# A graph kernel of two layers: epilogue operations of slabs 1 to 6 placed a step sooner or later, and other steps without partial sums

## The chip, the cores and the metric

The kernel runs on one core of a Trainium2 chip. The metric is the device time of one execution in microseconds (us). Before the change it is 233.94 us (median of three runs, 233.77 to 235.03). The engines are called PE (TensorE), DVE (VectorE), ACT (ScalarE), POOL (GpSimd) and SP (SyncE).

## The reference, cut to what matters

x has 4096 rows of 64, adj is 4096 x 4096 with zeros and ones.

```python
# layer 0
support = x @ W0
rank = cumsum(adj, axis=1); deg = rank[:, -1:]
k = minimum(deg, 100); pos = rank - (deg - k)
w = adj * where(pos > 0, 0.5 ** (k - pos), 0)
x1 = layernorm(x + w @ support + b0)
# layer 1
deg1 = maximum(sum(adj, axis=1) + 1, 1)
h = (adj @ x1 + x1) / deg1
z = concat([x1, h], axis=1) @ W1 + b1
u = relu(z); u = u / maximum(norm(u, axis=1), 1e-12)
out = layernorm(x1 + u)
```

So every one of the 16.8 million entries of adj is used three times: for a count of ones to its right, for a weight 0.5 to the power of that count, and for the plain sum of neighbours in layer 1. Layer 1 of any row needs x1 of all its neighbours, in all slabs.

## The kernel before, in words

The 4096 rows are cut into 8 slabs g of 512 rows, and the 4096 columns into 8 blocks k of 512, so there are 64 steps (g, k). Within a slab the blocks go from k = 7 down to 0, because the count runs from the right. Step i is numbered 0 to 63; slab g has steps 8g to 8g + 7. One load per step (512 KB in SBUF, issued on POOL's queue, line 109, converted to bf16 on its way) brings the transposed block of adj into one of 33 buffers `a16`. A buffer becomes free when its four matmuls of layer 1 are done.

A step's work for layer 0, `weigh`: 16 matmuls with `tri` (line 351) and 16 with `mine` (line 360) fill two PSUM tiles `v`, the exponents; ACT turns the first half and DVE the second half into the bits of bf16 weights `w` (lines 367 and 368, 1.1 and 1.2 us). `gather` (line 378, four matmuls) multiplies them with x, kept as high and low halves in fp16. It runs one step behind: `held` is the step before. The running count is made a chunk of steps ahead: `count` (line 321), then a DVE addition to the count so far (`cs`, lines 331 and 333), a matmul that spreads it over the partitions (`rep`, line 339), and an ACT operation (`near`, line 341) whose result `mine` reads. A chunk is one step in slabs 0 to 2, one or two in slab 3, two in slab 4, four in slabs 5 and 6, and two, two, four in slab 7.

Layer 1 begins long before layer 0 is done: `some_sums` takes, in each step, up to QUOTA = 4 matmuls (line 387; called a unit here) from a list `todo`, which `jobs` spells out: a pair (g, [k...]) says that slab g's sum over these blocks is made in one go in one PSUM bank. The first sum of a slab is copied out by ACT (line 406), later ones are added by DVE (line 403). The sums of one slab over block k need x1 of slab k, with the flag `low_at` telling from which step. No unit is issued in the steps of SAVED. The list is worked off in order: an entry that isn't ready holds back all behind it.

When a slab's last gather is done its epilogue runs, spread over the next steps as hooks. `at(i, engine, fn, g)` places a function at a step and an engine's slot, and the table PLACES (line 39) overrides step and slot by name. In the program, a step runs in this order: hooks of ACT, one load, hooks of POOL, the counts, hooks "DVE, early", `weigh`, hooks "ACT, late", the unit, `spread`, the eviction of a partial sum, `gather`, `first_hT`, hooks of PE, hooks of DVE. Each engine executes its instructions in program order.

The epilogue of slabs 2 to 6 (HALVED): `first_hT` copies the gathered sum (line 477), `half_sum` adds its low half (481), `half_high`, `half_rest` (488), `half_low` split it into fp16 parts in `x1T`, `half_degree` and `half_degree_out` (499) count the row's neighbours, `half_pz` multiplies by W0 and W1 (505), `half_y` adds x and an early part of layer 1 (510, 512). Then for all slabs: `first_mv` (bn statistics, 456 and 458), `first_s` (root, 427), `first_r` (four small operations, 433 to 437), `half_scale` (516), `first_x1` (four tensor_scalar operations that normalise, 565, on POOL for slabs 0 to 3 and on DVE for the others), `first_hi` (570), `first_xl` (575), `first_lo` (578), which split x1 for layer 1, `first_least` (552, 553), and `half_b1` (523), `half_c1` (527), `half_c1_b1` (531) on POOL. Slabs 0 and 1 transpose x1 instead, by `first_px` (583), `first_x1T` (586), `first_pu`, `first_c1`, `times_degree`.

At the start, `split_x` (221, 223 on POOL) and `split_x_low` (226 on DVE) split a block of x in each of steps 0 to 7, and `prepare` (229, 230 on POOL) scales W0, which has to have been loaded. After step 63 comes a tail in an order written out by hand, which ends the program. The change leaves that order as it is.

The slots of a step, in the code:

```python
run(i, ACT); load_next(); run(i, POOL)
for s in share: count(*s, s == ahead[0], s == ahead[-1])
run(i, "DVE, early")
w = w or weigh(g, k, nr)
run(i, "ACT, late")
done = some_sums(i, 0 if i in SAVED else QUOTA)
# at a chunk's last step: half of gather(*held) if no unit was issued, then spread
if done is not None: evict_part(done)
# rest of gather(*held); first_hT at a slab's first step
run(i, PE); run(i, DVE)
```

Of the kernel before, what the change touches and what calls it, by code (L numbers as in the profile page):

```python
# [17 lines left out]
PE = mybir.EngineType.PE  # L18
ACT = mybir.EngineType.Activation
DVE = mybir.EngineType.DVE  # L20
POOL = mybir.EngineType.Pool
# [14 lines left out]
QUOTA = 4  # L36
EARLY = 3
HALVED = range(2, 7)
PLACES = {"centered_parts": (9, POOL), "prepare": (5, POOL), "bias_columns": (7, POOL), "prepare_wx": (10, POOL), "half_c1_b1 3": (38, POOL), "half_c1_b1 4": (46, POOL), "half_c1_b1 5": (57, POOL), "half_c1_b1 6": (62, POOL), "products_parts": (10, POOL), "first_mv 0": (10, "DVE, early"), "first_r 0": (11, "DVE, early"), "first_least 0": (13, "DVE, early"), "first_s 0": (11, ACT), "first_pu 0": (16, PE), "times_degree 0": (18, POOL), "first_least 1": (20, DVE), "first_pu 1": (24, PE), "first_mv 2": (28, DVE), "first_s 2": (29, ACT), "first_r 2": (29, DVE), "half_scale 2": (29, DVE), "first_x1 2": (30, POOL), "first_hi 2": (31, ACT), "first_xl 2": (31, POOL), "first_lo 2": (32, ACT), "first_least 2": (31, DVE), "half_high 2": (26, ACT), "half_rest 2": (26, DVE), "half_degree_out 2": (26, DVE), "half_degree 2": (26, PE), "half_low 2": (27, ACT), "half_pz 2": (27, PE), "half_y 2": (27, DVE), "first_x1 3": (37, POOL), "first_hi 3": (38, "ACT, late"), "first_least 3": (38, "DVE, early"), "half_low 3": (34, ACT), "half_b1 3": (38, POOL), "half_c1 3": (37, POOL), "first_s 4": (44, ACT), "half_scale 4": (45, "DVE, early"), "first_xl 4": (46, POOL), "first_least 4": (45, DVE), "first_lo 4": (47, "ACT, late"), "half_low 4": (42, ACT), "half_b1 4": (46, POOL), "first_s 5": (52, ACT), "half_scale 5": (53, DVE), "first_hi 5": (54, "ACT, late"), "first_least 5": (57, DVE), "half_low 5": (50, ACT), "half_b1 5": (52, POOL), "half_c1 5": (55, POOL), "first_s 6": (60, ACT), "first_xl 6": (62, POOL), "first_lo 6": (62, "ACT, late"), "half_low 6": (58, ACT)}
LAG = 1  # L40
SAVED = (15, 17, 18, 21, 27)


@with_exitstack
def adj_resnorm_kernel(
# [23 lines left out]
    nc = tc.nc  # L69
# [317 lines left out]
        nc.tensor.matmul(acc, lhsT=x1hl[:, b, :], rhs=A[g][b // KB][:, b % KB, :], start=first, stop=last)  # L387


    jobs = [(0, [0]), (1, [0]), (0, [1]), (2, [0, 1]), (1, [1]), (3, [1, 0, 2]), (1, [2]), (0, [2]), (2, [2]), (4, [2, 1, 0, 3]), (1, [3]), (2, [3]), (0, [3]), (5, [3, 2, 1, 0, 4]), (3, [3, 4]), (6, [4, 3, 2, 1, 0, 5]), (4, [4, 5]), (1, [4, 5]), (0, [4, 5]), (2, [4])]  # L390
    acc1 = {}

    todo = [(g, k * KB + q, (k, q) == (ks[0], 0), (k, q) == (ks[-1], KB - 1)) for g, ks in jobs for k in ks for q in range(KB)]
# [14 lines left out]
    def some_sums(i, n):  # L408

        done = None  # L410
        while n and todo and done is None and ready(i, todo[0][0], todo[0][1]):
            g, b, first, last = todo.pop(0)
            if first:
                acc1[g] = ps_a.tile([P, R], F32, tag="acc1", name=f"acc_part_{g}_{b}")
            second(acc1[g], g, b, first, last)
            n -= 1
            if last:
                done = g
        return done
# [140 lines left out]

    def first_x1(g):
        mv, y, r = ep["mv", g], ep["y", g], ep["r", g]
        by = nc.gpsimd if g in [0, 1, 2, 3] else nc.vector
        for t in range(TB):
            by.tensor_scalar(  # L565
                x1[:, g * TB + t, :], y[:, t, :], mv[:, t, 0:1], r[:, t : t + 1], ALU.subtract, ALU.mult
            )
# [40 lines left out]
    def at(i, engine, fn, *args):  # L608
        i, engine = PLACES.get(" ".join([fn.__name__, *map(str, args)]), (i, engine))
        hooks[i, engine].append((fn, args))  # L610
# [35 lines left out]
    for g in range(NG - 1):  # L646
        i = NK * (g + 1)
        easy = POOL if g < EARLY else DVE
        late = 1 if g in HALVED else 0
# [3 lines left out]
            (3, "ACT, late", first_s, g),  # L653
            (3, DVE, first_r, g),
            (4, easy, first_x1, g),
            (5, ACT, first_hi, g),
            (5, easy, first_xl, g),
# [53 lines left out]
    for c, chunk in enumerate(chunks):  # L711
# [4 lines left out]
        for (g, k), share in zip(chunk, shares):  # L716
# [13 lines left out]
            n_todo = len(todo)  # L730
            done = some_sums(i, 0 if i in SAVED else QUOTA)
            half = 0
# [335 lines left out]
```

## Time and profile before

| what | value |
|---|---|
| median of three runs | 233.94 us (233.77, 233.94, 235.03) |
| the profiled execution's own time | 233.72 us |
| its span | 231.7 us |
| mean granted clock of PE | 0.975 |
| PE busy | 209.5 us (90%), 3138 instructions |
| DVE busy | 182.2 us (79%) |
| ACT busy | 140.6 us (61%) |
| POOL busy | 112.3 us (48%) |
| loads of adj, share of the 16 DMA engines | 73.7% |
| first weigh of step 16 / 32 / 40 | 55.45 / 99.33 / 122.40 us |
| the last load of adj lands | 174.75 us |

An engine's busy time leaves out waiting at its front, and matmuls are pipelined, with their ends modelled; a PE that is busy all the time is not necessarily at its peak. Shares over the whole span mix the 64 steps with a start and a tail that have other limits, so a step is read from its own stretch of the trace: from the first matmul of line 351 of one step to that of the next. In rows of the timeline the columns are start, duration (of one instruction, or of a run of equal ones), engine, line, operation, output and inputs, sizes, how many, and in brackets the idle time of the engine before it with what ended it.

### The profile page before, as it was taken

The page shows a single profiled execution, that of the slowest core. Times are in us where ns is not written, and L with a number is a line of the kernel's source. Part 1 is how long each engine was busy: PE and PEld are TensorE (multiplying, and loading weights), DVE is VectorE, ACT ScalarE, POOL GpSimd, SP SyncE. Part 2 cuts the span into 40 slices and gives each one's busy share as a digit, 9 for nine tenths or more (in the row PEclk, how much of TensorE's full clock was granted, in tenths as well). Part 3 has the DMA queues.
Part 4 walks back from the last instruction along what each step waited for, and adds up shares of the span by engine and source line. Part 5 has one row for each costly group of instructions (what it writes and reads, how often), then busy time and mean ns, then how long its engine had stood idle before and what let it go on. Part 6 is the DMA issues. An engine that isn't in the chain of part 4 may idle for free.

```text
span 231.7 us, 7494 instructions
## 1 busy us (share of the span) xinstructions
PE 209.5 (90%) x3138; PEld 95.2 (41%) x3178; DVE 182.2 (79%) x454; ACT 140.6 (61%) x212; POOL 112.3 (48%) x211
## 2 busy tenths in 40 slices
PE   7589999998998999999999999999999999999910
PEld 2133445443533443334333433443334344776810
DVE  6459877997797789798975996687678866599983
ACT  6057886687778767686557455664675451142684
POOL 7439677761537081641584056325433040079970
PEclk9799999999999999999999999999999999999975
DMA  6999999999999999999999999999970000000013
GB/s 201 209 213 219 215 216 213 217 217 214 215 219 212 214 214 223 211 214 214 218 217 207 200 183 210 204 195 181 205 168 4 3 0 0 3 0 1 23 45 113
DMA packets 11984, 37.36 MB, mean 161 GB/s; under 512 B 1328, under 2 KB 3504, under 8 KB 11952
## 3 DMA queue, kind: packets, MB, share of 16 engines
q0 software_dynamic: 9216, 33.56, 73.7%
q1 hardware_dynamic: 2736, 3.34, 4.7%
q8 instruction: 24, 0.39, 0.6%
q14 instruction: 8, 0.07, 0.1%
HBM read 69.40 MB, written 1.05 MB: 304 GB/s over the span
## 4 chain that ended last, share of the span: by engine, by line
PE 40%; DVE 11%; POOL 4%; ACT 3%; issue 2%; ACTq 0%; DVEq 0%; POOLq 0%
PE acc L378 12%; PE acc_part L387 11%; PE v L351 5%; PE cnt L321 3%; PE v L360 3%; ACT u L961 2%; POOL scratch L947 2%; DVE w L368 2%; POOL scratch L978 2%; DVE cs L331 1%; PE rep L339 1%; PE va L930 1%; PE pz L505 1%; PE vb L387 1%; DVE part L403 1%
## 5 line engine op out<-in xcount | busy, mean ns | idle before, releaser
L367 ACT ACTIVATE w<-v,less 128x1024 int16<-128x1024 f32 x64 | 71.3, 1113 | 43.7 <-PE v L360 31.7
L368 DVE TENSOR_SCALAR w<-v 128x1024 int16<-128x1024 f32 x64 | 78.2, 1221 | 13.0 <-PE v L360 12.1
L378 PE MATMUL acc<-w,xhl 128*128 128x512 bf16 x235 | 65.2, 380 | 1.9 <-issue 1.1
L109 POOL DMA_DIRECT2D a<-in_adjT_dram x64 | 36.9, 622 | 48.2 <-PE acc_part L387 25.4
L387 PE MATMUL acc_part<-a,x1hl 128*128 128x512 bf16 x140 | 38.2, 381 | 1.8 <-issue 1.3
L378 PEld LDWEIGHTS <-xhl 128*128 128x128 f16 x256 | 23.1, 98 | 33.6 <-issue 9.7
L341 ACT ACTIVATE near<-rep,most 128x512 bf16<-128x512 f32 x40 | 27.3, 682 | 8.7 <-PE rep L339 8.6
L387 PEld LDWEIGHTS <-x1hl 128*128 128x128 f16 x224 | 18.6, 98 | 31.1 <-issue 13.3
L351 PE MATMUL v<-a,tri 32*32 32x512 bf16 x1024 | 29.6, 384 | 0.3 <-DVE w L368 0.2
L360 PE MATMUL v<-near,mine 32*32 32x512 bf16 x1024 | 28.1, 376 | 0.0
L331 DVE TENSOR_TENSOR cs<-cnt,cs 128x512 bf16<-128x512 f32 x32 | 21.9, 686 | 4.4 <-PE cnt L321 4.0
L321 PE MATMUL cnt<-a,pick 128*32 128x512 bf16 x256 | 21.4, 389 | 4.2 <-DMA a<-in_adjT_dram 2.9
L351 PEld LDWEIGHTS <-tri 32*32 32x32 bf16 x1024 | 9.5, 87 | 21.7 <-issue 21.5
L339 PE MATMUL rep<-cs,further 128*128 128x512 bf16 x40 | 15.4, 385 | 1.5 <-DVE cs L331 1.1
L565 POOL TENSOR_SCALAR x<-y,mv_l,r_l 128x64 f32<-128x64 f32 x16 | 9.1, 575 | 12.4 <-DVE dr L516 6.4
L947 POOL TENSOR_TENSOR scratch<-scratch,power 128x4 f32<-128x4 f32 (+1 forms) x5 | 6.4, 1279 | 15.2 <-DVE scratch L949 15.1
L306 POOL TENSOR_TENSOR a<-a,ident_b 128x128 bf16<-128x128 bf16 x32 | 12.7, 431 | 0.1
L321 PEld LDWEIGHTS <-pick 128*32 128x32 bf16 x256 | 5.9, 94 | 14.8 <-issue 11.3
L333 DVE CAST cs<-cnt 128x512 bf16<-128x512 f32 x8 | 5.5, 692 | 7.8 <-PE cnt L321 7.8
L360 PEld LDWEIGHTS <-mine 32*32 32x32 bf16 x1024 | 10.2, 87 | 2.8 <-issue 2.4
L961 ACT ACTIVATE u<-u,scratch 128x64 f32<-128x64 f32 x27 | 9.8, 428 | 2.2 <-POOL scratch L980 2.1
L944 ACT ACTIVATE u<-u 128x256 f32<-128x256 f32 (+1 forms) x5 | 2.5, 502 | 12.1 <-DVE u L933 12.1
(177 smaller groups left out, 272.2 us busy)
## 6 DMA issues: line engine op xcount, KB each, us to landing
a<-in_adjT_dram POOLq DMA_DIRECT2D x64, 512.0 KB, 15.2
c<-in_x_quads_dram SPq DMA_DIRECT2D x2, 512.0 KB, 4.5
x<-in_x_dram SPq DMA_DIRECT2D x8, 128.0 KB, 7.2
out_dram<-u SPq DMA_DIRECT2D x8, 128.0 KB, 1.7
wts<-in_weights_dram SPq DMA_DIRECT2D x1, 192.5 KB, 7.2
```

The lines of the kernel that those rows point to most:

```text
L109: nc.gpsimd.dma_start(out=a, in_=adjT[g, k])
L321: nc.tensor.matmul(cnt[g][quarters[q], :], lhsT=pick[:, PW - 4 * k : PW - 4 * k + Q], rhs=A[g][k][:, q, :], start=first, stop=last,)
L331: nc.vector.tensor_tensor(new, cnt[g], cs[g], ALU.add)
L339: nc.tensor.matmul(pr, lhsT=further, rhs=cs[g], start=True, stop=True)
L341: nc.scalar.activation(near[g], pr, AF.Relu, bias=most, scale=-1.0)
L351: nc.tensor.matmul(v[e // 2][quarters[q], e % 2, :], lhsT=tri[quarters[e], :], rhs=A[g][k][quarters[e], q, :], start=True, stop=False,)
L360: nc.tensor.matmul(v[e // 2][quarters[q], e % 2, :], lhsT=mine[quarters[e], 4 * k + q, :], rhs=nr[quarters[e], :], start=False, stop=True,)
L367: nc.scalar.activation(w[:, 0:2, :], v[0], AF.Relu, bias=less)
L368: nc.vector.tensor_scalar(w[:, 2:4, :], v[1], -STEP * MAX_NEIGH, 0.0, ALU.add, ALU.max)
L378: nc.tensor.matmul(acc0[g], lhsT=xhl[:, b, :], rhs=w[:, q, :].bitcast(BF16), start=(k, q) == (NK - 1, 0), stop=(k, q) == (0, KB - 1),)
L387: nc.tensor.matmul(acc, lhsT=x1hl[:, b, :], rhs=A[g][b // KB][:, b % KB, :], start=first, stop=last)
L961: nc.scalar.activation(o[:, t, :], y[:, t, :], AF.Identity, bias=off[:, t : t + 1], scale=r[:, t : t + 1])
```

## The change

It edits three tables and one condition. In PLACES some operations get another step or another slot ("late" and "early" mean the other side of the weigh's conversions); `first_x1` of slabs 2 and 3 goes to DVE; SAVED and the order of `jobs` change. No arithmetic is added or removed. PLACES is one line in the code; here one changed entry stands on a line, and where an entry is missing on one side the default of `at` holds there, which is given in the comment.

```diff
 # the start, slabs 0 and 1
-prepare (5, POOL)                   +prepare (4, POOL)
-prepare_wx (10, POOL)               +prepare_wx (12, POOL)
-products_parts (10, POOL)           +products_parts (9, POOL)
-times_degree 0 (18, POOL)           +times_degree 0 (19, POOL)
-first_least 1 (20, DVE)             +first_least 1 (22, "DVE, early")
                                     +first_px 1 (23, PE)              # was 22
                                     +first_x1T 1 (24, ACT)            # was 23
                                     +first_c1 1 (25, DVE)             # was 24
                                     +times_degree 1 (29, POOL)        # was 25
 # slab 2
-half_low 2 (27, ACT)                +half_low 2 (27, "ACT, late")
-first_x1 2 (30, POOL)               +first_x1 2 (30, DVE)
-first_least 2 (31, DVE)             +first_least 2 (32, DVE)
                                     +half_b1 2 (30, POOL)             # was 29
                                     +half_c1 2 (31, POOL)             # was 30
                                     +half_c1_b1 2 (33, POOL)          # was 31
 # slab 3
                                     +half_sum 3 (33, DVE)             # was 32
                                     +half_high 3 (34, "ACT, late")    # was 33
                                     +half_rest 3 (34, DVE)            # was 33
                                     +half_degree 3 (34, PE), half_degree_out 3 (34, DVE)  # were 33
-half_low 3 (34, ACT)                +half_low 3 (35, ACT)
                                     +half_pz 3 (35, PE), half_y 3 (35, DVE)  # were 34
                                     +first_mv 3 (36, DVE)             # was 35
                                     +first_s 3 (37, "ACT, late")      # was 36
                                     +first_r 3, half_scale 3 (37, DVE)  # were 36
-first_x1 3 (37, POOL)               +first_x1 3 (38, DVE)
-first_hi 3 (38, "ACT, late")        +first_hi 3 (39, ACT)
-first_least 3 (38, "DVE, early")    +first_least 3 (39, DVE)
                                     +first_xl 3 (39, "DVE, early")    # was 38, DVE
                                     +first_lo 3 (39, "ACT, late")     # was 39, ACT
-half_c1 3 (37), half_c1_b1 3 (38)   # now 38 and 39
 # slabs 4, 5, 6
-first_s 4 (44, ACT)                 # now 44, "ACT, late"
-half_scale 4 (45, "DVE, early")     # now 44, DVE
-first_least 4 (45, DVE)             +first_least 4 (46, "DVE, early")
-first_lo 4 (47, "ACT, late")        # now 47, ACT
-half_b1 4 (46, POOL)                +half_b1 4 (42, POOL)
-first_s 5 (52, ACT)                 # now 52, "ACT, late"
-half_scale 5 (53, DVE)              +half_scale 5 (53, "DVE, early")
-first_hi 5 (54, "ACT, late")        # now 54, ACT
                                     +first_xl 5 (54, "DVE, early")    # was 54, DVE
                                     +first_lo 5 (55, "ACT, late")     # was 55, ACT
-first_least 5 (57, DVE)             +first_least 5 (58, "DVE, early")
-half_b1 5 (52), half_c1 5 (55), half_c1_b1 5 (57)   # now 51, 54, 56
-first_lo 6 (62, "ACT, late")        # now 63, ACT
                                     +first_least 6 (61, DVE)          # was 62
-half_c1_b1 6 (62, POOL)             # now 63
 
-SAVED = (15, 17, 18, 21, 27)
+SAVED = (15, 18, 26, 28)
-    jobs = [(0, [0]), (1, [0]), (0, [1]), (2, [0, 1]), (1, [1]), (3, [1, 0, 2]), (1, [2]), (0, [2]), (2, [2]), (4, [2, 1, 0, 3]), (1, [3]), (2, [3]), (0, [3]), (5, [3, 2, 1, 0, 4]), (3, [3, 4]), (6, [4, 3, 2, 1, 0, 5]), (4, [4, 5]), (1, [4, 5]), (0, [4, 5]), (2, [4])]
+    jobs = [(0, [0]), (1, [1]), (2, [0, 1]), (1, [0]), (0, [1]), (3, [1, 0, 2]), (2, [2]), (1, [2]), (0, [2]), (4, [2, 1, 0, 3]), (0, [3]), (2, [3]), (1, [3]), (5, [3, 2, 1, 0, 4]), (3, [3, 4]), (6, [4, 3, 2, 1, 0, 5]), (4, [4, 5]), (0, [4, 5]), (1, [4, 5]), (2, [4])]
-        by = nc.gpsimd if g in [0, 1, 2, 3] else nc.vector
+        by = nc.gpsimd if g in [0, 1] else nc.vector
```

With both tables the program issues its first units (slab and block) in these steps. Before: (0, 0) in 16, (1, 0) in 19, (0, 1) in 23, (2, 0) in 24, (2, 1) in 25, (1, 1) in 26. After: (0, 0) in 16, (1, 1) in 23, (2, 0) in 24, (2, 1) in 25, (1, 0) in 27, (0, 1) in 29. From step 30 on both issue one unit in the same steps, with the slabs in another order in a few of them.

More of the change, by code (lines that the diff above doesn't have):

```diff
@@ L38 @@
 HALVED = range(2, 7)
-PLACES = {"centered_parts": (9, POOL), "prepare": (5, POOL), "bias_columns": (7, POOL), "prepare_wx": (10, POOL), "half_c1_b1 3": (38, POOL), "half_c1_b1 4": (46, POOL), "half_c1_b1 5": (57, POOL), "half_c1_b1 6": (62, POOL), "products_parts": (10, POOL), "first_mv 0": (10, "DVE, early"), "first_r 0": (11, "DVE, early"), "first_least 0": (13, "DVE, early"), "first_s 0": (11, ACT), "first_pu 0": (16, PE), "times_degree 0": (18, POOL), "first_least 1": (20, DVE), "first_pu 1": (24, PE), "first_mv 2": (28, DVE), "first_s 2": (29, ACT), "first_r 2": (29, DVE), "half_scale 2": (29, DVE), "first_x1 2": (30, POOL), "first_hi 2": (31, ACT), "first_xl 2": (31, POOL), "first_lo 2": (32, ACT), "first_least 2": (31, DVE), "half_high 2": (26, ACT), "half_rest 2": (26, DVE), "half_degree_out 2": (26, DVE), "half_degree 2": (26, PE), "half_low 2": (27, ACT), "half_pz 2": (27, PE), "half_y 2": (27, DVE), "first_x1 3": (37, POOL), "first_hi 3": (38, "ACT, late"), "first_least 3": (38, "DVE, early"), "half_low 3": (34, ACT), "half_b1 3": (38, POOL), "half_c1 3": (37, POOL), "first_s 4": (44, ACT), "half_scale 4": (45, "DVE, early"), "first_xl 4": (46, POOL), "first_least 4": (45, DVE), "first_lo 4": (47, "ACT, late"), "half_low 4": (42, ACT), "half_b1 4": (46, POOL), "first_s 5": (52, ACT), "half_scale 5": (53, DVE), "first_hi 5": (54, "ACT, late"), "first_least 5": (57, DVE), "half_low 5": (50, ACT), "half_b1 5": (52, POOL), "half_c1 5": (55, POOL), "first_s 6": (60, ACT), "first_xl 6": (62, POOL), "first_lo 6": (62, "ACT, late"), "half_low 6": (58, ACT)}
@@ new lines @@
+PLACES = {"centered_parts": (9, POOL), "prepare": (4, POOL), "bias_columns": (7, POOL), "prepare_wx": (12, POOL), "half_c1_b1 2": (33, POOL), "half_c1_b1 4": (46, POOL), "half_c1_b1 5": (56, POOL), "products_parts": (9, POOL), "first_mv 0": (10, "DVE, early"), "first_r 0": (11, "DVE, early"), "first_least 0": (13, "DVE, early"), "first_s 0": (11, ACT), "first_pu 0": (16, PE), "times_degree 0": (19, POOL), "first_least 1": (22, "DVE, early"), "first_px 1": (23, PE), "first_x1T 1": (24, ACT), "first_pu 1": (24, PE), "first_c1 1": (25, DVE), "times_degree 1": (29, POOL), "first_mv 2": (28, DVE), "first_s 2": (29, ACT), "first_r 2": (29, DVE), "half_scale 2": (29, DVE), "first_x1 2": (30, DVE), "half_b1 2": (30, POOL), "first_hi 2": (31, ACT), "first_xl 2": (31, POOL), "half_c1 2": (31, POOL), "first_lo 2": (32, ACT), "first_least 2": (32, DVE), "half_high 2": (26, ACT), "half_rest 2": (26, DVE), "half_degree_out 2": (26, DVE), "half_degree 2": (26, PE), "half_low 2": (27, "ACT, late"), "half_pz 2": (27, PE), "half_y 2": (27, DVE), "first_mv 3": (36, DVE), "first_s 3": (37, "ACT, late"), "first_r 3": (37, DVE), "half_scale 3": (37, DVE), "first_x1 3": (38, DVE), "first_hi 3": (39, ACT), "first_xl 3": (39, "DVE, early"), "first_least 3": (39, DVE), "first_lo 3": (39, "ACT, late"), "half_sum 3": (33, DVE), "half_high 3": (34, "ACT, late"), "half_rest 3": (34, DVE), "half_degree_out 3": (34, DVE), "half_degree 3": (34, PE), "half_low 3": (35, ACT), "half_pz 3": (35, PE), "half_y 3": (35, DVE), "half_b1 3": (38, POOL), "first_xl 4": (46, POOL), "first_least 4": (46, "DVE, early"), "half_low 4": (42, ACT), "half_b1 4": (42, POOL), "half_scale 5": (53, "DVE, early"), "first_xl 5": (54, "DVE, early"), "first_least 5": (58, "DVE, early"), "first_lo 5": (55, "ACT, late"), "half_low 5": (50, ACT), "half_b1 5": (51, POOL), "first_s 6": (60, ACT), "first_xl 6": (62, POOL), "first_least 6": (61, DVE), "half_low 6": (58, ACT)}
```

## The prediction

> **What bounds the kernel now.** The page comes first. TensorE (PE) is busy in 90% of the span and in nearly every slice from 5 us to 225 us, at a granted clock of 0.9 or more; VectorE (DVE) comes second.
>
> ```profile
> PE 209.5 (90%) x3138; PEld 95.2 (41%) x3178; DVE 182.2 (79%) x454; ACT 140.6 (61%) x212; POOL 112.3 (48%) x211
> PE   7589999998998999999999999999999999999910
> DVE  6459877997797789798975996687678866599983
> PEclk9799999999999999999999999999999999999975
> ```
>
> So a step normally costs what its matmuls cost, and it costs more where PE waits for DVE or ACT. A program step here is one weigh. A step without a unit of partial sums (four matmuls of line 387, 0.97 us in the chain of waits) lasts about 2.1 us, one with a unit 2.6 to 3.4 us, by how many counts and epilogue matmuls it has. Any epilogue operation that fits into the slack of its engine costs nothing. That slack is read next, in the windows view cut at the starts of the weighs. The stretches of steps 29, 31, 33 and 37:
>
> ```profile
> 91.23:93.37 2.14, 1.80 (x41) 0.64 (x38) 2.14 (x10) 1.35 (x3) 0.00 (x0) 1.00 1.09 220
> 96.70:99.33 2.63, 2.47 (x44) 1.00 (x42) 2.42 (x4) 2.17 (x3) 2.60 (x5) 1.00 1.06 212
> 101.42:104.46 3.04, 2.76 (x49) 1.28 (x47) 2.68 (x4) 2.51 (x5) 0.53 (x1) 1.00 1.07 214
> 113.45:116.38 2.93, 2.73 (x44) 0.99 (x41) 2.81 (x7) 1.80 (x2) 2.04 (x5) 1.00 1.04 223
> ```
>
> Columns: length, then busy time of PE, PEld, DVE, ACT, POOL, clock, DMA share, GB/s. Steps 31, 35 and 39 have the 44 matmuls of step 37 and last 2.63; step 37 is 0.3 longer, step 33 0.4 longer (five small matmuls more). In both DVE is nearly full. The timeline says with what: an operation of the epilogue stands in DVE's order ahead of the running count (line 331), and the matmul that spreads the count (line 339) follows it at once.
>
> ```profile
> 101.75 0.68 DVE L481 SCALAR_TENSOR_TENSOR hT<-hT 64x512 f32<-64x512 f32 x1 [0.33 <-ACT hT L477]
> 102.47 0.69 DVE L331 TENSOR_TENSOR cs<-cnt,cs 128x512 bf16<-128x512 f32 x1
> 103.21 0.38 PE L339 MATMUL rep<-cs,further 128*128 128x512 bf16 x1
> ...
> 114.25 0.31 DVE L516 TENSOR_TENSOR dr<-deg,r_l 128x4 f32<-128x4 f32 x1
> 114.48 0.68 DVE L331 TENSOR_TENSOR cs<-cnt,cs 128x512 bf16<-128x512 f32 x1
> 115.21 0.38 PE L339 MATMUL rep<-cs,further 128*128 128x512 bf16 x1
> ```
>
> **The change, part by part.** All sums are made against the profiled execution, 233.72 us (span 231.7 and 2.0 around it). The median of the runs shown is 233.94, 0.22 higher. About 0.5% (1.17 us) is what a measurement of this kernel can tell from no change: its own three runs spread over 0.54%.
>
> *A, prepare from step 5 to step 4.* POOL waits for the weights there:
>
> ```profile
> 25.81 0.39 POOL L229 TENSOR_SCALAR wts<-wts 64x64 f32<-64x64 f32 x1 [1.64 <-DMA wts<-in_weights_dram]
> ```
>
> Before, the wait follows step 5's load and its split of x. After, both stand behind it: load 0.6, cast 0.4 and difference 0.67 begin after 26.7 instead of 22.4, so the split ends at about 28.6 instead of 24.2. DVE's scaling (line 226, 27.54) waits for that split and stands ahead of the count at 28.33 and of the spread at 29.23: both about 0.4 later. Cover: DVE was idle 0.39 just before that count, already used up by the sum. The load itself goes out some 4 us later with six loads outstanding. Taken +0.4, ends 0 and +0.45. products_parts, prepare_wx and times_degree 0 move on POOL alone and are needed several steps later: nothing.
>
> *B, steps 19 to 23.* The unit of step 19 (0.97) goes to step 29, with an ACT copy of 0.58 (line 406). In step 19 DVE sets the pace anyway: w until 66.5, the root until 67.2, the count at 67.30; only about 0.1 is gained. Step 22 loses four transposes and the x1T copy ahead of ACT's w; w on ACT starts at 70.30, 72.62, 75.49, so its 2.87 against a cycle of 2.32 holds 0.55 that goes. Step 23 takes the transposes for about 0.25. Together −0.4. Ends: −1.5 (both removals count whole) and 0.
>
> *C, steps 26 to 27.* A unit moves one step on, one for one; half_low behind ACT's w costs nothing while its readers are late in the step. Taken 0, ends −0.3 and +0.6 (one ACT operation of 0.6 on the path).
>
> *D, step 29 and x1 of slab 2.* Step 29 receives the unit of 0.97. PE was idle 0.34 of its 2.14, and step 30 begins with further waits for buffers of v, together about 0.75. But DVE, full in that step, also gets the partial-sum addition (line 403, 0.68), and in step 30 x1: 0.97 on DVE instead of 2.26 on POOL. DVE's idle 1.06 us before 96.82 takes most of that. The x1 rows:
>
> ```profile
> 94.62 2.26 POOL L565 TENSOR_SCALAR x<-y,mv_l,r_l 128x64 f32<-128x64 f32 x4 [6.39 <-DVE dr L516]
> 138.38 0.97 DVE L565 TENSOR_SCALAR x<-y,mv_l,r_l 128x64 f32<-128x64 f32 x4
> 138.34 0.57 POOL L109 DMA_DIRECT2D a<-in_adjT_dram  x1 [0.29 <-PE acc_part L387]
> 98.90 1.23 DVE L553 TENSOR_TENSOR least<-least 128x4 f32<-128x4 f32 x1
> ```
>
> The last, on 128x4 values, takes 0.16 elsewhere; it ran beside two POOL operations (98.74 to 100.10), and w on DVE at 100.19 came right behind it. After, it stands in step 32, where POOL has nothing but loads: 1.0 of DVE time goes, though only 0.2 of it delayed w. Taken +0.3 in all, ends +0.2 and +0.8.
>
> The third row bears on x1 as well: a load was issued beside x1 on DVE in 0.57, against 0.53 alone, so the sum carries 0.04 for it, hidden. The Trainium skill ("SBUF — State Buffer", "Who interferes with whom") speaks against the move: a DVE tensor_scalar in a two-port mode holds the port pair that it shares with GpSimd, and its box on loads issued from the GpSimd queue says that descriptors cannot be written meanwhile. By that rule each load issued beside x1 would be late by up to the 0.97 of x1, and the sum up to 1.94 higher for two slabs if the loads set the pace; the row speaks for 0.04 and the queue of loads (R3) for nothing.
>
> *E, step 33.* half_sum of slab 3 goes from step 32 to 33, behind the count: the 0.68 of line 481 and its wait for ACT no longer stand before 102.47. Step 33 falls from 3.04 to about 2.63. Taken −0.4, ends −0.4 and 0.
>
> *F, slab 3 in steps 34 to 40.* Every link is one step later. Step 37's count has the statistics (0.9) ahead of it instead of the roots (1.3 in all) and an addition: −0.3 by the windows above. The statistics cost +0.1 at step 36's end; x1 on DVE in step 38 uses idle time of 0.32 to 0.60 in steps 38 and 39. Taken −0.2, ends −0.3 and +0.3.
>
> *G, slabs 4 to 6.* lo, hi, dr and xl change sides of the weigh; DVE's half of w comes 0.3 to 0.7 later in steps 45, 46, 54 and 62, and DVE idles 1.4 us soon after each (from 123.19, 142.35 and 167.56). If that cover were gone, +0.6. Taken +0.1, ends 0 and +0.6.
>
> Sum: 0.4 − 0.4 + 0 + 0.3 − 0.4 − 0.2 + 0.1 = −0.2, so 233.5 on the profiled execution and 233.7 on the median; I forecast 233.6. The ends sum to −2.3 and +2.75, but not all fall one way.
>
> **The rivals.** *R1, faster.* The removals count whole and the additions fall into slack: A +0.2, B −1.5, D +0.2, E −0.4, F −0.3, the rest 0, together −1.8: about 232.0. For it: ACT, not DVE, may have set steps 19 to 23, and a unit shifted away from the slow ones helps in full. Against it: DVE's rows at 66.4 to 67.97 have no gap longer than 0.1.
>
> *R2, slower.* DVE becomes the bound behind x1. The place is the half of w right after x1, in steps 30 to 31 and 38 to 39; the price is 0.97 twice, 1.94; the point from which it decides is less than 0.97 of DVE idle time before the next count. With the forecast's other terms (−0.2): about +1.7, 235.5. For it: step 29 has DVE at 2.14 of 2.14 and now adds 0.68. Against: the idle 1.06 before 96.82 and the waits in steps 38 to 40, and POOL's 2.26 no longer delays hi on ACT (which waited 1.26 there).
>
> *R3, loads late.* Two units that free buffers for loads 37 and 38 come in steps 27 and 29 instead of 19 and 26. If the queue ran dry, each would cost up to 2.45, the spacing of landings. But load 37 was issued at 85.41 and landed at 104.22: 19 us of queue. At worst the issue moves by 5. It would give about 236, and is nearly excluded.
>
> **How the numbers follow.** Forecast case 0.42, R1 0.35, R2 0.21, R3 0.02. The forecast case lies within 0.5% of 233.94 (232.8 to 235.1), R1 below it, R2 and R3 above: faster 0.35, same 0.42, slower 0.23. The range reaches past R1's 232.0 by a little, since B to F could add up, and to just short of R2's value: 231.8 to 235.4.
>
> **What would show it.** In the changed profile: the spread of 29.23 at about 29.65 (A); step 19 near 3.1 and not 2.2 (B; 2.2 would be R1); step 29 near 2.9 and step 30 no longer (D; a DVE without idle time before the count in step 31 would be R2); step 33 at 2.63 (E); step 37 at 2.63 (F); `least` back at 0.16. Landings of the loads stay 2.45 apart to load 41. I am wrong if the tail from the last weigh, 43.5 us with its order unchanged, differs in length, or if steps outside 5 to 40 differ by more than 0.6 together.

## The result and the profile after

| | before | after |
|---|---|---|
| median of 22 runs each, same chips | 233.75 us | 234.61 us |
| ratio, 95% interval | | 1.0037 (1.0025 to 1.0048) |
| the profiled execution: time, span | 233.72, 231.7 us | 234.80, 232.7 us |
| start of step 39 / 54 / 63 | 119.77 / 161.17 / 186.54 us | 119.97 / 161.65 / 187.53 us |

The change makes the kernel slower by 0.87 us or 0.37%. That lies inside the predicted range and within the 0.5% called the same, but the forecast was 0.3 us faster, and the interval excludes that. The last step begins 0.99 us later and the tail is as long as before, so the steps account for all of it: 0.20 by step 39, 0.28 from there to step 54, 0.73 in step 54, and −0.23 in step 57 (the remainder is rounding).

The page after, beside the one in the prediction, shows PE and DVE busy for longer, though no arithmetic was added. For PE that says little: both kernels run the same matmuls, with 3178 weight loads in each trace, so the 40 more in the count of after (3178 against 3138) are records that the trace of before lacks. DVE took over the 8 operations of x1 from POOL, which take 0.97 for four where nothing holds them, 1.9 us together; its busy time grew by 4.6. The chain of what ended last (its shares by engine) has an item that was not there before, DMA. The first fence is of after, the second is the chain of before:

```profile
PE 214.4 (92%) x3178; PEld 95.7 (41%) x3178; DVE 186.8 (80%) x462; ACT 139.9 (60%) x212; POOL 107.6 (46%) x203
...
PE 36%; DVE 7%; DMA 4%; POOL 4%; ACT 3%; issue 1%; ACTq 0%; DVEq 0%; POOLq 0%
```

```profile
PE 40%; DVE 11%; POOL 4%; ACT 3%; issue 2%; ACTq 0%; DVEq 0%; POOLq 0%
```

The windows of steps 29, 31, 33 and 37 after the change, columns as in the prediction:

```profile
91.23:93.89 2.66, 2.66 (x45) 1.02 (x41) 2.66 (x11) 1.85 (x3) 0.69 (x2) 1.00 1.04 213
96.85:99.72 2.87, 2.79 (x45) 0.99 (x41) 2.78 (x6) 1.73 (x3) 1.57 (x4) 1.00 1.04 208
101.92:104.57 2.65, 2.65 (x46) 1.01 (x42) 2.56 (x5) 2.14 (x4) 0.69 (x2) 1.00 1.09 218
113.64:116.27 2.63, 2.63 (x46) 0.99 (x42) 2.56 (x11) 1.83 (x3) 1.66 (x4) 1.00 1.09 234
```

Steps 33 and 37 fell to 2.65 and 2.63, as forecast (E and F), and step 29 took in its unit for 0.5 us more. Yet step 39 begins no sooner. The chain of waits, in order of time, for the stretch around 119 us says why:

```profile
109.53 10.07 DMA a<-in_adjT_dram
119.60 0.04 issue
119.65 0.40 PE cnt L321 x4
120.05 0.36 PE v L351 x16
```

Load 43 was issued at 109.53 and landed at 119.60; the 10.07 us between stand in the queue of loads. The count that step 39 begins with looks a whole chunk ahead, over steps 40 to 43, and its last four matmuls need that load. The timeline of the count (line 321) shows the wait inside its duration; the first row is of before, the second of after:

```profile
118.80 1.05 PE L321 MATMUL cnt<-a,pick 128*32 128x512 bf16 x16
```

```profile
118.68 1.36 PE L321 MATMUL cnt<-a,pick 128*32 128x512 bf16 x16
```

In the kernel before, load 43 landed at 119.39, just as its matmuls came up: no wait, and no margin either.

The second thing to see is in DVE's and POOL's rows of the timeline after, with one of PE at the end:

```profile
118.20 2.46 DVE L565 TENSOR_SCALAR x<-y,mv_l,r_l 128x64 f32<-128x64 f32 x4
118.74 0.63 POOL L523 TENSOR_TENSOR b<-wts,deg 128x256 f32<-128x256 f32 x1
119.32 0.61 POOL L527 TENSOR_TENSOR c<-c,dr 128x256 f32<-128x256 f32 x1
...
122.51 0.74 POOL L311 TENSOR_TENSOR x<-x,wts 128x256 f32<-128x256 f32 x1
122.68 1.29 DVE L552 TENSOR_SCALAR least<-deg 128x4 f32<-128x4 f32 x1
123.20 0.73 POOL L531 TENSOR_TENSOR c<-c,b 128x256 f32<-128x256 f32 x1
...
159.32 1.26 DVE L434 SCALAR_TENSOR_TENSOR q_l<-q_l,eps_ln,mv_l 128x4 f32<-128x4 f32 x1
159.36 1.57 POOL L306 TENSOR_TENSOR a<-a,ident_b 128x128 bf16<-128x128 bf16 x4
...
161.11 1.22 DVE L368 TENSOR_SCALAR w<-v 128x1024 int16<-128x1024 f32 x1
...
162.38 0.43 PE L351 MATMUL v<-a,tri 32*32 32x512 bf16 x14 [0.34 <-DVE w L368]
```

x1 takes 0.97 alone, `least` 0.16 and the second operation of a root 0.22. Each is longer than that by 1.0 to 1.5 us, with 1.2 to 1.6 us of POOL's operations beside it. The last pair, with the order of DVE behind it, makes w of step 53 about a microsecond late, PE waits for the buffer of v that this w reads (the last row), and step 54 lasts 3.69 instead of 2.96.

So two theories were formed and tested. **L**: the stream of loads fixes when step 39 begins, and nothing won before it counts, nor anything lost that the wait for load 43 still covers. **P**: DVE and POOL hold each other up, and the change moved operations beside each other. Rivals: **O**, the order on DVE alone; R2 of the prediction, x1 on DVE; and A's price.

### The profile page after: what moved, and what is told of

It reads as the page before. It is cut to its first block, busy times and chain, and to the rows that moved or that the text cites. A ratio compares the mean times of both kernels' runs of the same rounds, so it can differ in the third digit from the quotient of the medians.

```text
span 232.7 us, 7538 instructions
## 1 busy us (share of the span) xinstructions
PE 214.4 (92%) x3178; PEld 95.7 (41%) x3178; DVE 186.8 (80%) x462; ACT 139.9 (60%) x212; POOL 107.6 (46%) x203
## 3 DMA queue, kind: packets, MB, share of 16 engines
HBM read 69.40 MB, written 1.05 MB: 303 GB/s over the span
## 4 chain that ended last, share of the span: by engine, by line
PE 36%; DVE 7%; DMA 4%; POOL 4%; ACT 3%; issue 1%; ACTq 0%; DVEq 0%; POOLq 0%
PE acc_part L387 10%; PE acc L378 10%; DMA a<-in_adjT_dram 4%; PE v L351 4%; PE cnt L321 3%; PE v L360 3%; ACT u L961 2%; POOL scratch L947 2%; POOL scratch L978 2%; PE va L930 1%; PE rep L339 1%; DVE w L368 1%; PE vb L387 1%; PE ma L387 1%; POOL scratch L979 1%
## 5 line engine op out<-in xcount | busy, mean ns | idle before, releaser
L378 PE MATMUL acc<-w,xhl 128*128 128x512 bf16 x256 | 69.2, 380 | 0.0
L387 PE MATMUL acc_part<-a,x1hl 128*128 128x512 bf16 x156 | 40.4, 382 | 0.1
L351 PE MATMUL v<-a,tri 32*32 32x512 bf16 x1024 | 30.3, 384 | 0.8 <-DVE w L368 0.8
L570 ACT CAST x1hl<-x 128x256 f16<-128x256 f32 x8 | 3.2, 405 | 12.1 <-DVE x L565 6.8
L575 POOL TENSOR_TENSOR xl<-x,x1hl 128x256 f32<-128x256 f32 x5 | 3.4, 676 | 12.4 <-ACT x1hl L570 12.3
```

The lines of the kernel that those rows point to most:

```text
L351: nc.tensor.matmul(v[e // 2][quarters[q], e % 2, :], lhsT=tri[quarters[e], :], rhs=A[g][k][quarters[e], q, :], start=True, stop=False,)
L378: nc.tensor.matmul(acc0[g], lhsT=xhl[:, b, :], rhs=w[:, q, :].bitcast(BF16), start=(k, q) == (NK - 1, 0), stop=(k, q) == (0, KB - 1),)
```

## The experiments

All times are medians beside runs of the kernel before on the same chips, with the ratio and its 95% interval. The edits are to the changed kernel unless said otherwise.

**e1, the root of slab 5 ahead of the weigh.**

```diff
+"first_s 5": (52, ACT)
```

> The changed kernel with one entry put back: the square root of slab 5 on ACT ahead of the weigh of step 52 instead of behind it. In the changed kernel step 54 lasts 3.69 us (2.96 before): DVE's root of slab 5 starts at 158.95 and its second operation takes 1.26 us (0.22 elsewhere) beside POOL's addition of the identity to the adjacency block (line 306), and with the product dr ahead of the weigh's conversion, w on DVE of step 53 starts at 161.11. Theory P (DVE and POOL hold each other up, and the moves put them side by side): the root is over before POOL's addition begins, no operation over 0.4 us, step 54 at 2.96, the whole 0.7 us faster than the changed kernel. Theory O (only the order on DVE counts: dr ahead of w): the root is earlier too, so it says the same here; the next kernel parts them. A theory in which only the loads' landings count: no change in the time.

234.26 us, ratio 1.0013 (1.0003 to 1.0024): a little faster than the changed kernel, half of the 0.7 us expected, since step 54 fell only to 3.45. The root began 0.14 earlier and still met POOL: now its last operation was held.

```profile
159.35 1.57 POOL L306 TENSOR_TENSOR a<-a,ident_b 128x128 bf16<-128x128 bf16 x4
159.52 1.05 DVE L437 SCALAR_TENSOR_TENSOR r_l<-s_l,q_l 128x4 f32<-128x4 f32 x1
```

In the kernel before, the same operation began 0.24 after POOL's and took 0.23; here it began 0.17 after POOL's and took 1.05. The rows of before:

```profile
158.81 1.58 POOL L306 TENSOR_TENSOR a<-a,ident_b 128x128 bf16<-128x128 bf16 x4
159.05 0.23 DVE L437 SCALAR_TENSOR_TENSOR r_l<-s_l,q_l 128x4 f32<-128x4 f32 x1
```

The collision is a matter of phase, which an expectation from the order alone could not give.

**e2, POOL's work moved away, DVE's order kept.**

```diff
+"add_self 5": (55, POOL)
```

> The changed kernel with POOL's addition of the identity for slab 5 (line 306, 1.57 us) in step 55 instead of 52; DVE's order stays as it is. Theory P: the second operation of slab 5's root falls from 1.26 to about 0.22, w of step 53 starts near 160.1, step 54 at 2.96 to 3.1, the whole 0.6 to 0.7 us faster than the changed kernel. Theory O: nothing changes, since DVE's order is the same: step 54 stays at 3.69.

The root's second operation took 0.22 and step 54 lasted 2.96, as P said and O did not. The total hardly moved, 234.53 us, ratio 1.0032 (1.0019 to 1.0045), because POOL, busier in steps 55 and 56, now held the half sum of slab 6: 1.43 instead of 0.68. Step 57 grew from 2.89 to 3.63. The collision had moved, not gone. Both rows of this run:

```profile
159.02 0.22 DVE L434 SCALAR_TENSOR_TENSOR q_l<-q_l,eps_ln,mv_l 128x4 f32<-128x4 f32 x1
...
170.26 1.43 DVE L481 SCALAR_TENSOR_TENSOR hT<-hT 64x512 f32<-64x512 f32 x1 [1.06 <-ACT hT L477]
```

**e3, x1 of slabs 2 and 3 back on POOL.**

```diff
-        by = nc.gpsimd if g in [0, 1] else nc.vector
+        by = nc.gpsimd if g in [0, 1, 2, 3] else nc.vector
-"first_x1 2": (30, DVE), "first_x1 3": (38, DVE)
+"first_x1 2": (30, POOL), "first_x1 3": (38, POOL)
```

> The changed kernel with x1 of slabs 2 and 3 back on POOL, in steps 30 and 38. In the changed kernel these run on DVE in 1.53 and 2.46 us beside POOL work, where 0.97 was expected. Theory R2 of the prediction (x1 on DVE is what costs): 0.9 to 1.9 us faster. Theory L (the stream of adjacency loads sets when step 39 begins: load 43 lands at 119.60 in the changed kernel and step 39 begins 0.37 later; 119.39 and 0.38 before): step 39 still begins 0.37 to 0.38 after the landing of load 43, whatever the steps before it do, and the whole stays within 0.3 us of the changed kernel.

235.35 us, ratio 1.0057 (1.0042 to 1.0073): slower than with x1 on DVE. R2's mechanism falls. Step 39 kept to L (load 43 landed at 119.50, step 39 began at 119.87). The loss of 0.7 us against the changed kernel was more than the 0.3 expected: x1 of slab 3 came later, xl was held to 0.97, and step 40 grew from 2.65 to 3.15.

**e4, the load of x for slab 4 later.**

```diff
+"load_x 4": (40, POOL), "add_b0 4": (41, POOL)
```

> The changed kernel with the load of x for slab 4 (128 KB) issued in step 40 instead of 35, and the addition of b0 to it in step 41 instead of 39: no engine has less to do before step 39, but the stream of loads does. Theory L: load 43 lands 0.3 to 0.6 us earlier, the count of step 38 no longer waits for it (1.05 instead of 1.36 us), and step 39 begins some 0.3 us earlier; POOL's addition of b0 also leaves the side of the DVE operation that took 1.29 us at 122.68, so up to 0.3 more may come from P in step 40. Without L: step 39 begins when it did, 119.97.

Load 43 landed at 119.23, 0.37 earlier, and step 39 began at 119.60, 0.37 earlier: L. The total was 236.26 us, ratio 1.0091 (1.0073 to 1.0109), which was a mistake of the experiment: x of slab 4 was issued only at 125.10, too late for the sum y of step 42, and step 43 grew from 2.63 to 3.99.

**e5, the start as before.**

```diff
-"prepare": (4, POOL), "prepare_wx": (12, POOL), "products_parts": (9, POOL), "times_degree 0": (19, POOL)
+"prepare": (5, POOL), "prepare_wx": (10, POOL), "products_parts": (10, POOL), "times_degree 0": (18, POOL)
```

> The changed kernel with the start of the kernel before: prepare in step 5, prepare_wx in 10, products_parts in 10, times_degree 0 in 18. The prediction's part A gave the change +0.4 us for prepare alone. Theory A: 0.4 us faster than the changed kernel, and step 39 begins that much earlier. Theory L: step 6 begins 0.37 to 0.4 after load 7 lands or a little later, step 12 loses its extra 0.1 to 0.2, and all of it is gone by step 39, which begins 0.37 to 0.38 after load 43 lands; the whole differs only by what load 43's landing differs, at most 0.25.

234.49 us, ratio 1.0024 (1.0009 to 1.0039). This is the clearest trace of L. Step 38 began at 115.54, 0.73 earlier than in the changed kernel, and step 39 at 120.05, later by 0.08. The 0.73 is not the price of the start: step 38 began at 115.97 in e9 and at 116.48 in e10, which are the same kernel up to there, so executions alone differ by up to 0.9 here. The count stood still for the difference:

```profile
117.95 0.83 PE L321 MATMUL cnt<-a,pick 128*32 128x512 bf16 x12
119.72 0.40 PE L321 MATMUL cnt<-a,pick 128*32 128x512 bf16 x4 [0.93 <-DMA a<-in_adjT_dram]
120.05 0.43 PE L351 MATMUL v<-a,tri 32*32 32x512 bf16 x16
```

**e6, two collisions taken away.**

```diff
-"half_c1_b1 2": (33, POOL), "first_least 3": (39, DVE)
+"half_c1_b1 2": (32, POOL), "first_least 3": (41, DVE)
```

> The changed kernel with two POOL collisions taken away: the addition of b1 to c1 of slab 2 (line 531) in step 32 instead of 33, so that it doesn't stand beside the half sum of slab 3 (1.67 us in the changed kernel, 0.68 alone), and `least` of slab 3 in step 41 instead of 39, away from POOL's two additions (1.29 us instead of 0.16). Theory P: both fall to 0.68 and 0.16; steps 33 to 35 are some 0.4 us shorter together, and steps 40 and 41 last 2.41 and 2.49 as before the change. Theory L with P: the first gain ends at step 39, which begins 0.37 after load 43 all the same; only the second is kept: 0.2 to 0.35 faster than the changed kernel. Without L: 0.6 to 0.8 faster.

234.55 us, ratio 1.0022 (1.0007 to 1.0038), hardly to be told from the changed kernel. The half sum fell from 1.67 to 0.68, but steps 33 to 35 kept their 2.65, 3.04 and 3.08 to the hundredth: that collision had cost nothing, and the expected 0.4 was wrong. `least` was back at 0.16; steps 40 and 41 together lost 0.18, of which step 42 gave back 0.10.

**e7, slab 5 as before.**

```diff
+"first_s 5": (52, ACT), "half_scale 5": (53, DVE), "first_hi 5": (54, "ACT, late"), "first_least 5": (57, DVE)
+"half_b1 5": (52, POOL), "half_c1 5": (55, POOL), "half_c1_b1 5": (57, POOL)
-"first_xl 5": (54, "DVE, early"), "first_lo 5": (55, "ACT, late")
```

> The changed kernel with the nine entries of slab 5 as before. Theory P (with the place of dr ahead of w as its second half): step 54 is back at 2.96 instead of 3.69, the whole 0.5 to 0.75 us faster than the changed kernel, so within 0.35 of the kernel before. If the rest of the change in steps 40 to 63 matters more than this stretch: less than 0.3.

234.01 us, ratio 1.0001 (0.9984 to 1.0018): no loss is left that the interval shows, though in the trace the last step still begins 0.32 later than before the change. Step 54 is back at 2.96; step 57 at 3.12, because POOL meets the half sum of slab 6 again (0.92), as it did before.

**e8, slab 5 counted in chunks of 2, 2 and 4 steps.**

```diff
-{3: [1, 1, 2, 2, 2], 4: [2, 2, 2, 2], 7: [2, 2, 4]}
+{3: [1, 1, 2, 2, 2], 4: [2, 2, 2, 2], 5: [2, 2, 4], 7: [2, 2, 4]}
```

> The changed kernel with slab 5 counted in chunks of 2, 2 and 4 steps instead of 4 and 4: the count made in step 38 needs loads 40 and 41 only, not load 43, at the price of one more spread (matmul, DVE copy or addition, ACT operation). Theory L: step 38 no longer waits, and step 39 begins at about 119.2 (3.71 less 0.31 of waiting and 0.44 for eight counts that move two steps on), before load 43 lands (119.6); afterwards 0.44 and some 0.3 to 0.5 for the spread come back in steps 39 to 42, so the whole lies between 0.3 us faster and 0.5 slower. Without L: step 39 begins only 0.44 earlier, at 119.5, and the whole is slower.

Step 39 began at 119.37, before load 43 landed (119.73), which no kernel with chunks of four did. The extra spread cost more than estimated: steps 39 to 42 grew by 1.45 in all. 235.25 us, ratio 1.0066 (1.0040 to 1.0091).

**e9, the fixes together.**

```diff
+"prepare": (5, POOL), "prepare_wx": (10, POOL), "products_parts": (10, POOL), "times_degree 0": (18, POOL)
+"first_least 3": (41, DVE), "add_self 5": (51, POOL), "first_s 5": (52, ACT), "half_scale 5": (53, DVE)
```

> The changed kernel with the start of the kernel before, `least` of slab 3 in step 41, the root of slab 5 on ACT ahead of the weigh of step 52, dr of slab 5 behind that of step 53, and POOL's addition of the identity for slab 5 in step 51, where DVE only has statistics and a conversion from PSUM. Theories L and P together: the 0.7 us won at the start are gone at step 39, which begins 0.37 to 0.38 after load 43 lands; steps 40 and 41 lose 0.18, step 54 is back at 2.96, step 57 stays at 2.89: 0.8 to 0.9 us faster than the changed kernel, ratio to the kernel before 0.998 to 1.000.

233.62 us, ratio 0.9993 (0.9980 to 1.0006), as expected. POOL's 1.57 us for slab 5 now begin as the statistics (line 456) end, run beside line 458, and hold up nothing (0.59 and 0.36 are what the two take elsewhere):

```profile
155.80 0.59 DVE L456 BATCH_NORM_STATS2 st_l<-y 128x6 f32<-128x64 f32 x4
156.31 0.36 DVE L458 BATCH_NORM_AGGREGATE mv_l<-st_l 128x2 f32<-128x6 f32 x4
156.33 1.57 POOL L306 TENSOR_TENSOR a<-a,ident_b 128x128 bf16<-128x128 bf16 x4
```

**e10 and e11, slab 5 in chunks of 3 and 5, on e9 and on the kernel before.**

```diff
+5: [3, 5]
```

> The same with slab 5 counted in chunks of 3 and 5 steps instead of 4 and 4: as many spreads as now, but the count made in step 38 needs loads 40 to 42 (the last landed at 117.20 in the changed kernel) and no longer load 43. Theory L: step 39 begins at about 118.8, before load 43 lands, and the gains of the steps before it are kept: about 1.1 us faster than the kernel with the fixes alone, ratio to the kernel before 0.994 to 0.996. Without L: as the kernel with the fixes alone.

> The kernel before with slab 5 counted in chunks of 3 and 5. In the kernel before the count of step 38 met load 43 just as it landed (1.05 us, no waiting). Theory L: nothing to be won, step 39 begins at 119.6 to 119.8, ratio to the kernel before 0.999 to 1.001. If the other division of the chunks were itself what makes the kernel with it faster: as much faster here, 0.995.

Both were slower, and both expectations failed: 234.71 us, ratio 1.0044 (1.0032 to 1.0056), and 234.94 us, 1.0062 (1.0043 to 1.0081). In e10 step 39 began at 119.65, before load 43 landed (119.83), but the chunk of five needs load 47 for the count that step 42 begins with, and that became the next wait (the step was counted one too late when this was planned):

```profile
129.57 0.40 PE L321 MATMUL cnt<-a,pick 128*32 128x512 bf16 x4 [0.58 <-DMA a<-in_adjT_dram]
129.90 0.43 PE L351 MATMUL v<-a,tri 32*32 32x512 bf16 x16
```

Load 47 landed at 129.53 there and at 129.48 in e11, and step 42 began 0.37 later in both. L holds, at another load.

**e12, e9 with the load of x for slab 4 in step 38.**

```diff
+"load_x 4": (38, POOL), "add_b0 4": (40, POOL)
```

> The kernel with the fixes, and the load of x for slab 4 issued in step 38 instead of 35, with b0 added to it in step 40 (in an earlier run with it in step 40 and 41, load 43 landed 0.37 us earlier, but x then came too late for the first layer's sum in step 42). Theory L: load 43 lands 0.2 to 0.4 us earlier than in the kernel with the fixes, at 119.0 to 119.2, and step 39 begins 0.37 to 0.38 later; x is there in time, so this is kept: 0.2 to 0.4 us faster than the kernel with the fixes, ratio to the kernel before 0.997 to 0.999. Without L: step 39 begins at 119.8 as in the kernel with the fixes, ratio 0.999 to 1.000.

Load 43 landed at 119.21 and step 39 began at 119.58, as L said, but the gain was not kept: the total was 233.68 us, ratio 0.9997 (0.9984 to 1.0009). Step 42 had grown from 4.07 to 4.57, behind a new collision:

```profile
125.28 0.72 POOL L311 TENSOR_TENSOR x<-x,wts 128x256 f32<-128x256 f32 x1 [0.57 <-DMA x<-in_x_dram]
125.36 1.18 DVE L481 SCALAR_TENSOR_TENSOR hT<-hT 64x512 f32<-64x512 f32 x1 [1.13 <-ACT hT L477]
```

**e13, the same with the two apart.**

```diff
-"add_b0 4": (40, POOL), "first_least 3": (41, DVE)
+"add_b0 4": (41, POOL), "first_least 3": (40, DVE)
```

> The kernel of the run before with b0 added to x of slab 4 in step 41 instead of 40 and `least` of slab 3 in step 40 instead of 41. In the run before, step 39 began 0.25 us earlier than in the kernel with the fixes, and step 42 gave 0.50 back: POOL's addition of b0 began at 125.28, and DVE's half sum beside it took 1.18 us instead of 0.68. Theory P: apart, the half sum takes 0.68 and step 42 lasts 3.8 to 4.1 us; with load 43 landing at 119.2 the whole is 0.2 to 0.5 us faster than the kernel with the fixes, ratio to the kernel before 0.997 to 0.9985. If it was x of slab 4 arriving late, step 42 stays at 4.5 or longer, since b0 is now added still later, and the ratio is 1.000 or above.

233.22 us, ratio 0.9972 (0.9962 to 0.9983): faster than both kernels. The half sum took 0.68, step 42 4.07, and load 43's earlier landing was kept.

The measure of L, from the step starts of the traces:

| kernel | step 38 begins | load 43 lands | step 39 begins | difference of the last two |
|---|---|---|---|---|
| before | 116.38 | 119.39 | 119.77 | 0.38 |
| after | 116.27 | 119.60 | 119.97 | 0.37 |
| e2 | 115.76 | 119.62 | 120.00 | 0.38 |
| e5 | 115.54 | 119.67 | 120.05 | 0.38 |
| e9 | 115.97 | 119.45 | 119.83 | 0.38 |
| e13 | 115.53 | 119.23 | 119.61 | 0.38 |
| e8 | 116.41 | 119.73 | 119.37 | −0.36 |

Step 38 begins anywhere within 0.9 us; step 39 follows the landing to a hundredth, except where the chunk does not ask for that load. In e1, e3, e4, e6, e7 and e12, which are not in the table, the difference is 0.37 or 0.38 too. In the kernel before, it is so without a wait.

## Why the prediction was right or wrong

The traces put the last step 0.99 us later, where the forecast's sum says 0.2 sooner. Of these 1.2 us, 0.5 arise up to the start of step 39 (A to F were to give −0.3 and gave +0.20) and 0.7 behind it (G, with the end of F, was to give +0.1 and gave +0.79).

**A to F as terms of PE's own time: sums about right, single steps not always.** A: in the kernels with prepare in step 4 whose first weigh did not begin early, step 6 lasts 3.23 to 3.53, against 2.87 to 2.94 with it in step 5, the gather waiting for DVE's line 226: 0.3 to 0.7, forecast 0.4. In the profiled execution of the changed kernel the first weigh began 1.43 us earlier than before, and loads, not the split, held steps 3 to 5; the same is seen in e9 with the old start (first weigh at 10.90, step 6 at 28.58), so it goes with the execution and not with the change. The sign named for A, the spread of 29.23 at about 29.65, came out (29.70), but by these loads: that was luck. B with C, steps 19 to 28: −0.63, forecast −0.4; step 19 became 2.48, nearer to R1's 2.2 than to the 3.1 of the forecast, so it gained 0.7 where 0.1 was named, and step 20 gave 0.4 of it back. D, steps 29 to 32: +0.50, forecast +0.3, of which `least` is back at 0.16 but x1 took 1.53 beside POOL's addition of b0. E: −0.39, forecast −0.4. F, up to step 38: −0.22 without the 0.31 of waiting, forecast −0.2.

**The step that failed first: R3.** The prediction dismissed the loads because load 37 waited 19 us between issue and landing, and called that a queue far ahead. That is no margin. Landings in this stretch (loads 37 to 43) are 2.4 to 2.9 us apart in both traces, whenever the load was issued: load 43 went out 0.25 sooner after the change (109.53 against 109.78) and landed 0.2 later. The margin is the time from a landing to the first use. That was never read for the count, which looks up to four steps ahead: load 43 landed at 119.39 and was used at once. So the sum A to F could not shorten the kernel at all: in the changed kernel 0.31 us of it went into the wait for load 43, and in e5 0.73 us of an earlier step 38 did. What the path kept of the terms up to there is +0.20, the difference of two landings (119.60 and 119.39), not of the terms. The check that was offered, "Landings of the loads stay 2.45 apart to load 41", watched the right queue for the wrong thing. Why the landing differs by 0.2 was not settled: with the start of the kernel before and x loaded where it was, load 43 landed between 119.39 and 119.92 (the kernel before, e5, e9, e10, e11).

**The step that failed in size: G, and the end of F.** G was put at +0.1 with an end of +0.6 if the cover was gone; steps 54 to 62 gave +0.51, of which step 54 alone +0.73, and the cause was not the one priced. The cover named, DVE's idle time after the weigh, was there. What the prediction left out is who else was at work when the moved operation ran: POOL's 1.57 us of line 306 beside the root. It had the sign of this in hand, `least` at 1.23 instead of 0.16, and used it for that one operation, not for the root of slab 5, x1 and `least` of slab 3. The last of these cost 0.2 in steps 40 and 41, with 0.1 left behind step 42 (e6); the half sum's 1.67 cost nothing (e6). x1 of slab 3 stands in the wait for load 43, and behind it nothing is seen of it either: in e13, where it took 2.26, steps 39 to 42 last 11.61 together, as before the change. Step 57's −0.23 is the same effect with the other sign. Of the 0.28 between steps 39 and 54, no run accounts for the other 0.2.

**R1 and R2.** R1 priced B at −1.5; steps 19 to 28 gave −0.63, and no gain there could have reached the end. R2's mechanism, x1 on DVE, is refuted by e3. Its sign was right by luck; its place and its price were not. The range owes its upper end to R2, so that it holds the result is luck too.

**The Trainium skill's rule.** "SBUF — State Buffer", "Who interferes with whom" was weighed for one direction only, a DVE operation that keeps POOL from issuing loads. For x1 the traces show nothing of that, though they hardly test it: the load at 118.19 began just ahead of x1 at 118.20 and was issued in 0.53, and the one load in the two traces that began within an x1 on DVE (before, 160.91, x1 of slab 5 from 160.69) in 0.59. The other direction is what the runs show, with 1.26 instead of 0.22 (line 434) and 1.43 instead of 0.68 (line 481). The same section says that a DVE operation with two SBUF inputs contends with a GpSimd operation that reads SBUF, and both lines are such operations. It also says that a DVE operation with at most one SBUF input, outside the two-port modes, does not contend with GpSimd; the statistics, if they count as such, fit that, with 0.59 for four beside POOL's line 306 (after, 113.26), as elsewhere.

## What to carry to other kernels

Before adding up what single steps gain, look for the places where a steady stream of loads meets its consumer: compare each landing with the first use of that buffer, look-ahead uses included. A long time from issue to landing (19 us for load 37, 10 us for load 43 here) says that the stream is busy, not that it is early, and a gain ahead of a meeting point without margin is worth nothing. When an operation moves in a kernel where DVE and POOL share the work, check what the other engine does at that time, and read durations, not only idle time: the held operations here show as long ones (1.26 instead of 0.22), with no idle time before them.

## What the runs showed of the hardware that was not expected

- A DVE operation on 128 x 4 values took 1.05 to 1.29 us beside two to four POOL operations in a row, each of 0.4 to 0.75 (`least` of slab 3 up to 1.80 in e2 and e5), so it was held for longer than one of them; a shift of 0.07 us between the two (the kernel before and e1) went with 0.23 in one and 1.05 in the other.
- Moving one load of 128 KB of x out of the way let load 43 land 0.24 to 0.37 us earlier (119.23 in e4 against 119.60 after, 119.21 in e12 against 119.45 in e9); in no run with x where it was did it land before 119.39.
- The gain of the best version, e13, is 0.28%, from an earlier landing of one load and collisions avoided, with no work removed: in its trace step 39 begins 0.16 sooner than before the change, step 57 lasts 0.23 less, and the last step begins 0.35 sooner.
